# A decoder layer with 32 routed experts: the token lists computed by one-hot products, and the last shared sums stored from another queue

## The chip, the cores and the metric

One core of one Trainium2 chip runs the whole kernel. The metric is device time in microseconds (us). Times without a unit are microseconds from the start of the profiled span. TensorE is called PE, VectorE DVE, ScalarE ACT, GpSimd POOL and SyncE SP.

## What is computed

One decoder layer on 4096 tokens (2 x 2048) of width 512, in float32, in three residual steps. The first two are attention-like (stage 0 of the kernel: squared-relu scores against fixed weight keys; stage 1: cross-attention on 128 context tokens). The third is the one that matters here: a shared SwiGLU plus one of 32 routed SwiGLUs for each token.

```python
shared_out = silu(x @ sg) * (x @ su) @ sd            # 512 -> 1024 -> 512, all tokens
logits = x @ gate_w                                  # 32 experts
topk_ids = argmax(logits); scores = sigmoid(max(logits))
sorted_x = (x * scores)[argsort(topk_ids)]
d = grouped_mm(silu(grouped_mm(sorted_x, rg)) * grouped_mm(sorted_x, ru), rd)
out = x + shared_out + d[inverse order]
```

The number of tokens of each expert is known only when the kernel runs.

## The kernel before, in words

Every float32 matmul is done in fp32r as three products of rounded high and low parts (`three`). `split` (L89) makes the parts: ACT casts the high one (L94), and DVE or POOL subtracts for the low one (L97). The instructions of each engine stand in a fixed order, which a list scheduler decides when the kernel is built, with modelled costs. `later` shifts the priority of what is written inside it (positive: later). Tiles come from tagged slots in rotation (tags A to K, `raw` for loads, `W` with 45 slots); the first write of a tile waits until the users of the slot's former tile are done. PSUM has the banks P1 to P4, two buffers each.

The parts follow one another, with PE as the engine that is fed:

- **Stages 0 and 1** (to about 1450). Stage 1 writes for each token the index of its expert into `ef` (128 partitions x 32: token t*128+partition in column t), the scaled tokens `xs` to DRAM, and the residual `x2`.
- **Shared.** The first 1024 tokens go plainly (`plain_up`, `plain_down`). Three groups G of 1024 tokens follow, each in three steps p over 256 hidden columns, nine steps in all, of about 30 us each from 1511 on. A step does seven Strassen-like products (`up`, matmuls at L970). DVE adds the PSUM banks into `u` (L977, L980, L981) and `gu` (L991, L994), ACT applies silu, DVE multiplies by it (L958; one quarter is multiplied by POOL instead), and `split` gives hh and hl. After each product `between` gives one turn to several generators: the weights of the next step, splits of `z` and of the down weights, one `down` (L1002, bank P4) of the step before, which DVE adds into `acc` (L1008, slots W), and one stretch of `route` (it goes on at each `yield`). In the last step of a group `acc` is stored to `out` by SP's queue (L1010).
- **Route** (L623-772), inside the shared part. All values stand in 128 partitions x 32. `oh` is the token-by-expert table (128 x 32 x 32 bf16); five doubling additions give running sums; matmuls with a triangle and with ones (bank P4, L675, L681) give each token's place within its expert and the experts' totals. Experts are ranked by their number of tokens. Each rank has a fixed capacity `CAP` and first block `BASE`; what exceeds it goes to overflow blocks of 128. Tables of 128x1024 (L642, L644) and reductions over them (L648) select base, capacity, expert by rank and overflow offsets, which make up `plan` (97 integers that SP reads into registers: 32 experts by rank, 64 overflow experts, the number of overflow blocks). Operations of 128x512 (L731-741) and small ones (L744-755) give the address of each token. 32 indirect DMAs (L760, POOL) write the token numbers into four lists in DRAM, which four stores at the start had filled with 4096, a token that doesn't exist. SP loads the lists back (L767), DVE takes their minimum (L770), and `idx` (128 x blocks) and `ids` (its copy in DRAM for the overflow loop) are done.
- **Routed** with **Rest** woven in. Blocks of 256, 128 or 64 tokens of one expert: `gather` (L1192, an indirect DMA of POOL that reads `idx`) fetches `x` into slots of tag H, PE turns it (L1204; L1223 for blocks of 256), products (L1233, L1288), and an indirect DMA that adds into `out` (L1331). Weights are loaded by SP and split in `load` into rh and rl, whose slots are shared with `acc` (tag W). Rest does the last 256 hidden columns of the shared part (L1113, L1142) and adds its result `v` into `out` by POOL's queue (L1146).
- **Overflow** (L1416): a loop over the overflow blocks, its count from `plan[96]`.

Routed begins with these lines (L1385), where `blocks[0]` is Rest's first block and `blocks[1]` the first routed one, of 256 tokens, so two gathers:

```python
    with later(g, -200):
        prepare(*blocks[0])
        prepare(*blocks[1])
        turn_x(*blocks[0], "P3")
```

Of the kernel before, what the change touches and what calls it, by code (L numbers as in the profile page):

```python
# [8 lines left out]
F32 = mybir.dt.float32  # L9
FR = mybir.dt.float32r  # L10
# [25 lines left out]
NBLK = NB + NOV  # L36

# [585 lines left out]
def route(g, ef, tab, tri, lists, ids, plan, idx):  # L623
# [3 lines left out]

    room = []

    def small(name, dt=F32, n=E):  # L630
        if not room or room[-1][1] + n > 512:
            room.append([g.raw.tile([128, 512], F32, name="small", tag="raw"), 0])
        v, at = room[-1]
        room[-1][1] += n
        return v[:, at:at + n].bitcast(dt)
# [4 lines left out]
    def table(name, a, b, op, c=None, op2=None, tag="K"):  # L640
        w = big(name, tag)
        V.tensor_tensor(w[:], a, b, op)  # L642
        if c is not None:
            V.tensor_tensor(w[:], w[:], c, op2)  # L644
        return w

    def total(out, w):
        V.tensor_reduce(out, w, AX.X, A.add)  # L648

    consts = g.a.tile([128, 256], F32, name="consts", tag="m", bufs=2)  # L650
    nc.sync.dma_start(consts[:, 0:160], tab)
    iota, cst = consts[:, 0:64], consts[:, 64:160]
    io, basec, capc, tok = iota[:, 0:E], cst[:, 0:E], cst[:, E:2 * E], cst[:, 2 * E:3 * E]
    tri32 = g.tile("K", "tri32", F32, (128, 256))
    nc.sync.dma_start(tri32[:], tri)
    trib = g.tile("K", "trib", BF, (128, 256))
    V.tensor_copy(trib[:], tri32[:])

    yield

    oh = table("oh", bc(io, 1, E), bc(ef[:], 2, E), A.is_equal, tag="J")
# [7 lines left out]
    pos = [g.tile("G", "pos", F32, (128, 16, E)) for _ in range(2)]  # L669
    for hf in range(2):  # L670
        o = g.bank("P4", "rt", (128, 16, E))
        first = 1 - hf
        for w, x, t in ((0, oh, 0), (128, run, -1)):
            k = first if w else 0
            nc.tensor.matmul(o[:, k:, :].rearrange("p t e -> p (t e)"), trib[:, w:w + 128],  # L675
                             x[:, 16 * hf + t + k:16 * hf + 16 + t, :].rearrange("p t e -> p (t e)"),
                             start=w == 0, stop=w > 0, skip_group_check=True)
        nc.scalar.copy(pos[hf][:], o[:])
        yield
    o = g.bank("P4", "rt", (128, E))  # L680
    nc.tensor.matmul(o[:], trib[:, 128:256], run[:, E - 1, :], start=True, stop=True)  # L681
    tot, key, rank = small("tot"), small("key"), small("rank")
    V.tensor_copy(tot[:], o[:])
    yield

    V.tensor_scalar(key[:], tot[:], float(E), None, A.mult)
    V.tensor_tensor(key[:], key[:], io, A.subtract)
    total(rank[:], table("gt", bc(key[:], 1, E), bc(key[:], 2, E), A.is_gt)[:])
    yield
    ro = table("ro", bc(io, 1, E), bc(rank[:], 2, E), A.is_equal, tag="J")  # L690
    base, cap, er = small("base"), small("cap"), small("er")
    total(base[:], table("wb", ro[:], bc(basec, 1, E), A.mult)[:])
    total(cap[:], table("wc", ro[:], bc(capc, 1, E), A.mult)[:])
    yield
    total(er[:], table("we", ro[:].rearrange("p e r -> p r e"), bc(io, 1, E), A.mult)[:])
    V.tensor_copy(plan[:, 0:E], er[:])

    yield

    over, oi, nov = small("over"), small("oi", I32), small("nov", n=1)  # L700
    V.tensor_tensor(over[:], tot[:], cap[:], A.subtract)
    V.tensor_scalar(over[:], over[:], 0.0, 127.0, A.max, A.add)
    V.tensor_copy(oi[:], over[:])
    V.tensor_scalar(oi[:], oi[:], 7, None, A.arith_shift_right)
    V.tensor_copy(over[:], oi[:])
    total(nov[:], over[:])
    V.tensor_copy(plan[:, 96:97], nov[:])
    yield
    ovs, ove = small("ovs"), small("ove")
    total(ovs[:], table("lt", bc(io, 2, E), bc(io, 1, E), A.is_gt, bc(over[:], 1, E), A.mult)[:])  # L710
    V.tensor_tensor(ove[:], ovs[:], over[:], A.add)
    for hf in range(2):
        te = small(f"te{hf}")
        total(te[:], table("le", bc(iota[:, 32 * hf:32 * hf + 32], 2, E), bc(ove[:], 1, E), A.is_ge)[:])
        V.tensor_scalar(te[:], te[:], float(E - 1), None, A.min)
        yield
        V.tensor_copy(plan[:, 32 + 32 * hf:64 + 32 * hf], te[:])

    yield

    diff, blk, pt = small("diff"), small("blk"), small("pt")
    V.tensor_scalar(diff[:], ovs[:], float(NB), None, A.add)
    V.tensor_tensor(diff[:], diff[:], base[:], A.subtract)
    for hf in range(2):
        ts = slice(hf * 16, hf * 16 + 16)
        shape = [128, 16, E]
        capb, diffb, baseb = (v[:].unsqueeze(1).to_broadcast(shape) for v in (cap, diff, base))
        sel = g.tile("K", "sel", F32, (128, 16, E))
        past = g.tile("K", "past", F32, (128, 16, E))
        yield  # L730
        V.tensor_tensor(sel[:], pos[hf][:], capb, A.is_ge)  # L731
        V.tensor_tensor(past[:], sel[:], capb, A.mult)
        V.tensor_tensor(pos[hf][:], pos[hf][:], past[:], A.subtract)
        yield
        V.tensor_tensor(sel[:], sel[:], diffb, A.mult)
        V.tensor_tensor(sel[:], sel[:], baseb, A.add)
        V.tensor_tensor(sel[:], sel[:], oh[:, ts, :], A.mult)
        total(blk[:, ts], sel[:])
        yield
        V.tensor_tensor(pos[hf][:], pos[hf][:], oh[:, ts, :], A.mult)  # L740
        total(pt[:, ts], pos[hf][:])
    yield
    pi, hi = small("pi", I32), small("hi", I32)
    V.tensor_copy(pi[:], pt[:])  # L744
    V.tensor_scalar(hi[:], pi[:], 7, None, A.arith_shift_right)
    V.tensor_scalar(pi[:], pi[:], 127, None, A.bitwise_and)
    V.tensor_copy(pt[:], hi[:])
    V.tensor_tensor(blk[:], blk[:], pt[:], A.add)
    V.tensor_copy(pt[:], pi[:])
    V.tensor_scalar(pt[:], pt[:], float(NBLK), None, A.mult)  # L750
    V.tensor_tensor(blk[:], blk[:], pt[:], A.add)
    yield
    dst, toki = small("dst", I32), small("toki", I32)
    V.tensor_copy(dst[:], blk[:])
    V.tensor_copy(toki[:], tok)
    yield

    flat = [v[:].rearrange("p (b o) -> (p b) o", o=1) for v in lists]
    for t in range(E):
        nc.gpsimd.indirect_dma_start(out=flat[t % 4], out_offset=bass.IndirectOffsetOnAxis(ap=dst[:, t:t + 1], axis=0),  # L760
                                     in_=toki[:, t:t + 1], in_offset=None)
        if t % 2:
            yield
    parts = []
    for v in lists:
        parts.append(g.W.tile([128, NBLK], I32, name="list", tag="W"))
        nc.sync.dma_start(parts[-1][:], v[:])  # L767
    yield
    for v in parts[1:]:
        V.tensor_tensor(parts[0][:], parts[0][:], v[:], A.min)  # L770
# [784 lines left out]
```

## Time and profile before

| | us |
|---|---|
| median of three runs | 2704.23 (2700.75, 2704.23, 2708.0) |
| the profiled execution, its own time | 2703.28 |
| its span from first to last instruction | 2701.4 |
| mean granted clock of PE in it | 0.997 |
| routing on DVE: 73 instructions | 56.5 busy, mostly 1549-1641 |
| routing on POOL: 32 indirect DMAs | 31.4 busy, 1643-1722 |
| the list ready (`idx`) | 1725.3 |
| first gathers of routed tokens start | 1790.5, 1802.3, 1806.4, 1812.8 |
| the seam, from the last pair product to the first routed one | about 1800-1826 |

How the profile is read. A row of a group names line, engine, operation, tiles out<-in, shape and count, then busy time and the mean of one in ns. A row of a wait names the engine, what it wanted to do, after "<-" who released it, then the microseconds in total, how many times and the longest. "128x512 f32" is partitions x elements of a partition. A row of a timeline is start, duration, engine, line, operation; in brackets the idle time ahead of it and its releaser. An engine name with q (SPq) is that engine's instruction queue: DMA issues and semaphores. Matmul ends are modelled, so gaps on PE are best read from start to start.

The granted clock was 0.5 in three pieces of 3.413 us, at 1125.2, 1449.4 and 1824.9.

### The profile page before, as it was taken

To read this page: it belongs to the slowest core of one execution; us is meant where nothing else is said; L and a number is where in the kernel's file an instruction comes from. 1 tells how busy PE (TensorE), PEld (TensorE's weight loads), DVE (VectorE), ACT (ScalarE), POOL (GpSimd) and SP (SyncE) were. 2 spreads that over 40 slices of the span, in tenths; PEclk is the share of its full clock that TensorE was granted. 3 is DMA by queue.
4 is the path that set the end of the run, shared out by engine and by line. 5 is a ranking of instruction groups with operands and counts; after the bars stand their busy time and mean duration, and the time that the engine had idled before them with its cause. 6 is when DMAs were issued, how large, how long until landed. Compare 5 with 4: busy or idle time off the path is not lost. (4 is left out here: it accounts for less than half of the span.)

```text
span 2701.4 us, 47562 instructions
## 1 busy us (share of the span) xinstructions
PE 2641.7 (98%) x14629; PEld 2274.0 (84%) x14629; DVE 2071.4 (77%) x4703; ACT 1853.0 (69%) x4118; POOL 1132.2 (42%) x911
## 2 busy tenths in 40 slices
PE   7999999999999999999999999999999999999998
PEld 5878888887878999899997878778989898898886
DVE  7777777777777988888887487574777777778985
ACT  7788788888767777677785323343666676767885
POOL 5576565666644334344341457621122222212221
PEclk9999999999999999999999999999999999999999
DMA  4012112212021223323249846663889899999994
GB/s 154 32 63 86 55 67 81 81 47 76 30 87 34 80 76 130 103 92 107 79 143 338 289 142 238 218 211 108 261 282 281 281 305 299 295 284 291 323 319 148
DMA packets 269408, 446.66 MB, mean 165 GB/s; under 512 B 33536, under 2 KB 77568, under 8 KB 269152
## 3 DMA queue, kind: packets, MB, share of 16 engines
q1 hardware_dynamic: 254464, 416.46, 45.5%
q0 software_dynamic: 14688, 27.17, 4.9%
q8 instruction: 115, 1.88, 0.3%
q14 instruction: 141, 1.16, 0.1%
HBM read 348.83 MB, written 96.64 MB: 165 GB/s over the span
## 5 line engine op out<-in xcount | busy, mean ns | idle before, releaser
L97 DVE TENSOR_TENSOR rl<-raw,rh 128x512 fp32r<-128x512 f32 x768 | 487.7, 683 | 86.8 <-ACT rh L94 59.6
L94 ACT CAST rh<-raw 128x512 fp32r<-128x512 f32 x768 | 438.3, 621 | 138.5 <-DMA raw<-in_rg 89.2
L97 POOL TENSOR_TENSOR pl<-p,ph 128x512 fp32r<-128x512 f32 x320 | 411.3, 1296 | 263.2 <-ACT ph L94 206.5
L349 ACT ACTIVATE rl<-s 128x512 f32<-128x512 f32 x512 | 293.0, 604 | 38.1 <-PE s L345 32.8
L1331 POOL DMA_INDIRECT out_dram<-v,idx x46 | 114.7, 2492 | 457.7 <-ACT v L1329 367.4
L464 ACT ACTIVATE e<-e,nm 128x128 f32<-128x128 f32 x512 | 199.2, 391 | 70.4 <-DVE nm L461 70.1
L353 DVE TENSOR_TENSOR p<-s,rl 128x512 f32<-128x512 f32 x320 | 215.0, 682 | 40.6 <-ACT rl L349 38.2
L94 ACT CAST ph<-p 128x512 fp32r<-128x512 f32 x320 | 199.2, 626 | 63.1 <-DVE p L353 60.2
L467 POOL TENSOR_TENSOR e<-e,ri 128x512 f32<-128x512 f32 x128 | 133.2, 1042 | 215.0 <-DVE ri L465 103.3
L345 PE MATMUL s<-qh,kwl 128*128 128x512 f32 x512 | 205.7, 403 | 7.3 <-DVE p L353 4.1
L309 PE MATMUL o<-pl,vwh 128*128 128x512 f32 x512 | 202.8, 396 | 1.4 <-POOL pl L97 1.4
L309 PE MATMUL o<-ph,vwl 128*128 128x512 f32 x512 | 200.4, 393 | 0.9 <-ACT ph L94 0.9
L353 DVE TENSOR_TENSOR s<-s,rl 128x512 f32<-128x512 f32 x192 | 133.2, 694 | 88.3 <-ACT rl L349 87.8
L345 PE MATMUL s<-ql,kwh 128*128 128x512 f32 x512 | 200.1, 391 | 0.0
L345 PE MATMUL s<-qh,kwh 128*128 128x512 f32 x512 | 199.9, 390 | 0.0
L309 PE MATMUL o<-ph,vwh 128*128 128x512 f32 x512 | 199.7, 390 | 0.0
L970 PE MATMUL gu<-z,swh 128*128 128x512 f32 x504 | 157.3, 389 | 0.0
L438 PE MATMUL q<-yh,wql 128*128 128x256 f32 x512 | 149.5, 292 | 2.8 <-DVE v L497 2.4
L97 DVE TENSOR_TENSOR pl<-s,ph 128x512 fp32r<-128x512 f32 x192 | 131.0, 683 | 20.6 <-ACT ph L94 18.2
L438 PE MATMUL q<-yh,wqh 128*128 128x256 f32 x512 | 145.6, 284 | 0.0
L438 PE MATMUL q<-yl,wqh 128*128 128x256 f32 x512 | 145.0, 283 | 0.0
L97 POOL TENSOR_TENSOR vl<-v,vh 128x512 fp32r<-128x512 f32 x64 | 84.4, 1319 | 124.3 <-ACT vh L94 111.6
(361 smaller groups left out, 7996.1 us busy)
## 6 DMA issues: line engine op xcount, KB each, us to landing
raw<-in_rg SPq DMA_DIRECT2D x256, 256.0 KB
raw<-in_ru SPq DMA_DIRECT2D x256, 256.0 KB
raw<-in_rd SPq DMA_DIRECT2D x256, 256.0 KB
z<-zT SPq DMA_DIRECT2D x116, 256.0 KB
b<-x SPq DMA_DIRECT2D x40, 256.0 KB
raw<-in_sgu SPq DMA_DIRECT2D x39, 256.0 KB
swh<-wS SPq DMA_DIRECT2D x36, 256.0 KB
swl<-wS SPq DMA_DIRECT2D x36, 256.0 KB
```

Source lines behind the costliest of these rows:

```text
L94: g.nc.scalar.copy(hi, src)
L97: g.low = (lo_engine or g.nc.vector).tensor_tensor(lo, src, f32(hi), A.subtract)
L309: nc.tensor.matmul(o[:], w, y[:], start=kt == 0 and n == 0, stop=kt == 15 and n == 2)
L345: nc.tensor.matmul(s[:], w, y[:], start=n == 0, stop=n == 2)
L349: m0 = nc.scalar.activation(r[:], s[:], AF.Relu)
L353: m1 = nc.vector.tensor_tensor(p[:], s[:], r[:], A.mult)
L438: nc.tensor.matmul(o[:, i, :], part(w, k, p), y[k // 2][:, k % 2, :], start=n == 0, stop=n == 11)
L464: nc.scalar.activation(e[:, hs], e[:, hs], AF.Exp, bias=nm[:, h:h + 1], scale=0.125, accum_out=su[:, h:h + 1])
L467: nc.gpsimd.tensor_tensor(e4, e4, ri[:].unsqueeze(2).to_broadcast([128, 4, 128]), A.mult)
L970: nc.tensor.matmul(o[:], y, z, start=(at, x) not in begun, stop=j == 1 and m == 2, skip_group_check=True)
L1331: nc.gpsimd.indirect_dma_start(out=out, out_offset=bass.IndirectOffsetOnAxis(ap=idx[rows, b + j:b + j + 1], axis=0), in_=v[rows], in_offse ...
```

## The change

Four edits, in `route`, `down`, `gather` and the constants:

1. **Values by expert in 32 partitions.** Totals are made in two forms, as a row in all partitions and as a column of 32 partitions (two small matmuls). Rank, capacity, base, overflow are then [32,1] values or [32,32] tables; overflow offsets come from a matmul with the triangle. `plan` is made from one PSUM tile by a minimum (128x96) and one copy.
2. **One packed look-up.** Capacity, 8 x base and 512 x d (the distance to the overflow block) are put on the diagonals of three 32x32 bf16 tables and summed by three accumulated matmuls with ones into one row; each token picks its value by one 128x512 product with `oh` and a reduction for each half, and shifts and masks take it apart.
3. **Lists as one-hot products.** For each of 32 columns of tokens DVE makes `lt` (128x128: is this the token's slot?) and `rt` (128x128: is this its block? times the token's code), both in fp32r; PE multiplies them into P4, four columns in one accumulation, eight of these in all; DVE adds each 128x110 result into `acc`. A few more operations turn code into token number. The 32 indirect DMAs, the lists in DRAM, their loads and the four stores at the start are gone.
4. **Queue and slot.** The eight stores of the last group's `acc` go to POOL's queue; the gather of `blocks[1]` takes a slot of tag F instead of H.

The order of instructions is the same on every engine to the end of stage 1, but for SP's four stores and POOL's memset at the start. In the changed order the one-hot operations on DVE stand in one run of 16 and then in runs of 8. The diff, cut to its core (code that only goes is left out where the description above tells it; the constants too):

```diff
+    iota, capc, basec, code, own = (consts[:, a:b] for a, b in ((0, 128), (128, 160), (160, 192), (192, 224), (224, 225)))
+    io = iota[:, 0:E]
     tri32 = g.tile("K", "tri32", F32, (128, 256))
     nc.sync.dma_start(tri32[:], tri)
-    trib = g.tile("K", "trib", BF, (128, 256))
-    V.tensor_copy(trib[:], tri32[:])
-
+    tables = g.tile("G", "tables", BF, (128, 1024))
+    trib, ones = tables[:, 0:128], tables[:, 128:256]
+    V.tensor_copy(tables[:, 0:256], tri32[:])
+
+    ecol, ro, over_b, ge = (tables[0:E, a:b] for a, b in ((256, 384), (384, 416), (416, 448), (448, 512)))
+    diag = [tables[0:E, 512 + 32 * i:544 + 32 * i] for i in range(3)]
+    V.tensor_copy(ecol, own[0:E].to_broadcast([E, 128]))
...
+    of_all = g.bank("P4", "rt", (128, 64))
+    product(of_all[:, 0:E], ones, run[:, E - 1, :])
+    product(of_all[0:E, E:E + 2], run[:, E - 1, :], ones[:, 0:2])
+
+    tot, key, rank = (small(n, n=1, p=E) for n in ("tot", "key", "rank"))
+    keys, gt = (small(n, p=E) for n in ("keys", "gt"))
+    V.tensor_copy(tot, of_all[0:E, E:E + 1])
+    V.scalar_tensor_tensor(key, tot, float(E), own[0:E], A.mult, A.subtract)
+    V.scalar_tensor_tensor(keys, of_all[0:E, 0:E], float(E), io[0:E], A.mult, A.subtract)
+    V.tensor_tensor(gt, keys, key.to_broadcast([E, E]), A.is_gt)
+    total(rank, gt)
+    V.tensor_scalar(ro, io[0:E], rank, None, A.is_equal)
...
+        pos = g.tile("G", "pos", F32, (128, 16, E))
+        V.tensor_tensor(pos[:], o[:], oh[:, ts, :], A.mult)
+        total(pt[:, ts], pos[:])
...
+    cap, base, over, oi, ove, d = (small(n, n=1, p=E) for n in ("cap", "base", "over", "oi", "ove", "d"))
+    V.tensor_tensor(keys, ro, capc[0:E], A.mult)
+    V.tensor_tensor(gt, ro, basec[0:E], A.mult)
+    total(cap, keys)
+    total(base, gt)
+    V.scalar_tensor_tensor(over, cap, -64.0, tot, A.mult, A.add)
+    V.tensor_scalar(over, over, 0.0, 127.0, A.max, A.add)
+    oi = oi.bitcast(I32)
+    V.tensor_copy(oi, over)
+    V.tensor_scalar(oi, oi, 7, None, A.arith_shift_right)
+    V.tensor_copy(over, oi)
+    V.tensor_copy(over_b, over.to_broadcast([E, E]))
...
+    product(of_all[0:E, 0:E], trib[0:E, 0:E], over_b)
+    ovs = small("ovs", n=1, p=E)
+    V.tensor_copy(ovs, of_all[0:E, 0:1])
+    V.tensor_tensor(ove, ovs, over, A.add)
+    V.tensor_scalar(ge, iota[0:E, 0:64], ove, None, A.is_ge)
+    V.scalar_tensor_tensor(d, ovs, float(NB + 64), base, A.add, A.subtract)
+    for v, col, w in zip(diag, (cap, base, d), (1.0, 8.0, 512.0)):
+        V.tensor_scalar(v, g.ident[0:E, 0:E], col, w, A.mult, A.mult)
+    o = g.bank("P4", "rt", (128, 160))
+    product(o[:, 0:32], ecol, ro)
+    product(o[:, 32:96], ones[0:E], ge)
+    product(o[:, 96:98], ones[0:E], over_b[:, 0:2])
+    for i, v in enumerate(diag):
+        product(o[:, 128:160], ones[0:E], v, i, 2)
+    V.tensor_scalar(plan[:, 0:96], o[:, 0:96], float(E - 1), None, A.min)
+    V.tensor_copy(plan[:, 96:97], o[:, 96:97])
+
+    rec = small("rec")
+    for hf in range(2):
+        ts = slice(16 * hf, 16 * hf + 16)
+        sel = g.tile("G", "sel", F32, (128, 16, E))
+        V.tensor_tensor(sel[:], oh[:, ts, :], o[:, 128:160].unsqueeze(1).to_broadcast([128, 16, E]), A.mult)
+        total(rec[:, ts], sel[:])
...
+    ri, parts, blk = small("ri", I32), small("parts", I32, 3 * E), small("blk")
+    V.tensor_copy(ri, rec)
+    V.tensor_scalar(parts[:, 0:32], ri, 7, 6, A.bitwise_and, A.logical_shift_left)
+    V.tensor_scalar(parts[:, 32:64], ri, 3, 63, A.logical_shift_right, A.bitwise_and)
+    V.tensor_scalar(parts[:, 64:96], ri, 9, None, A.logical_shift_right)
+    pf = small("pf", n=3 * E)
+    V.tensor_copy(pf, parts)
+    past = rec
+    V.tensor_tensor(past, pt, pf[:, 0:32], A.is_ge)
+    V.scalar_tensor_tensor(blk, pf[:, 64:96], -64.0, past, A.add, A.mult)
+    V.tensor_tensor(past, past, pf[:, 0:32], A.mult)
+    V.tensor_tensor(pt, pt, past, A.subtract)
+    V.tensor_tensor(blk, blk, pf[:, 32:64], A.add)
+    at, atf = parts[:, 0:64], pf[:, 0:64]
+    V.tensor_copy(ri, pt)
+    V.tensor_scalar(at[:, 0:32], ri, 7, None, A.arith_shift_right)
+    V.tensor_scalar(at[:, 32:64], ri, 127, None, A.bitwise_and)
+    V.tensor_copy(atf, at)
+    V.tensor_tensor(blk, blk, atf[:, 0:32], A.add)
+    slot = atf[:, 32:64]
...
-    flat = [v[:].rearrange("p (b o) -> (p b) o", o=1) for v in lists]
-    for t in range(E):
-        nc.gpsimd.indirect_dma_start(out=flat[t % 4], out_offset=bass.IndirectOffsetOnAxis(ap=dst[:, t:t + 1], axis=0),
-                                     in_=toki[:, t:t + 1], in_offset=None)
-        if t % 2:
-            yield
-    parts = []
-    for v in lists:
-        parts.append(g.W.tile([128, NBLK], I32, name="list", tag="W"))
-        nc.sync.dma_start(parts[-1][:], v[:])
-    yield
-    for v in parts[1:]:
-        V.tensor_tensor(parts[0][:], parts[0][:], v[:], A.min)
-    V.tensor_copy(idx[:], parts[0][:, 0:NB])
-    nc.sync.dma_start(ids[:], parts[0][:])
+    acc = g.W.tile([128, NBLK], F32, name="list", tag="W")
+    for c in range(8):
+        lt, rt = g.tile("J", "lt", FR, (128, 4, 128)), g.tile("K", "rt", FR, (128, 4, 128))
+        with later(g, 30):
+            for i in range(4):
+                t = slice(4 * c + i, 4 * c + i + 1)
+                V.tensor_scalar(lt[:, i, :], iota, slot[:, t], None, A.is_equal)
+                V.tensor_scalar(rt[:, i, :], iota, blk[:, t], code[:, t], A.is_equal, A.mult)
+        yield
+        with later(g, 30):
+            o = g.bank("P4", "rt", (128, 128))
+            for i in range(4):
+                product(o[:], lt[:, i, :], rt[:, i, :], i, 3)
+            if c == 0:
+                V.tensor_copy(acc[:], o[:, 0:NBLK])
+            else:
+                V.tensor_tensor(acc[:], o[:, 0:NBLK], acc[:], A.add)
+        yield
+    none = g.W.tile([128, NBLK], F32, name="none", tag="W")
+    V.tensor_scalar(none[:], acc[:], 0.0, float(T - 2047), A.is_equal, A.mult)
+    V.scalar_tensor_tensor(acc[:], acc[:], 0.0, acc[:], A.is_lt, A.add)
+    out = g.W.tile([128, NBLK], I32, name="out", tag="W")
+    V.scalar_tensor_tensor(out[:], acc[:], 2047.0, none[:], A.add, A.add)
+    V.tensor_copy(idx[:], out[:, 0:NB])
+    nc.sync.dma_start(ids[:], out[:])
...
-            nc.sync.dma_start(out[r, :], b[:])
+            (nc.gpsimd if G == NG - 1 else nc.sync).dma_start(out[r, :], b[:])
...
-    def gather(b, r, m):
+    def gather(b, r, m, tag="H"):
-            x = g.tile("H", "x")
+            x = g.tile(tag, "x")
...
-        prepare(*blocks[1])
+        prepare(*blocks[1], "F")
...
-                empty = g.tile("A", "empty", I32, (128, NBLK))
-                nc.gpsimd.memset(empty[:], T)
-                for v in lists:
-                    nc.sync.dma_start(v[:], empty[:])
```

## The prediction

> **What bounds the kernel now.** I read the busy shares first.
>
> ```profile
> PE 2641.7 (98%) x14629; PEld 2274.0 (84%) x14629; DVE 2071.4 (77%) x4703; ACT 1853.0 (69%) x4118; POOL 1132.2 (42%) x911
> ```
>
> PE is the bound, and the change takes no matmul out of it. It can win only where PE stood still, and it loses what it adds to PE. So the second view is PE's waits, from the first routing step (1580) to just behind the seam between the shared and the routed part (1860).
>
> ```profile
> PE pt L1204 <- DMA x<-xs,idx: 2.1, 1, 2.1
> PE gu L970 <- DVE u L977: 2.1, 1, 2.1
> PE d L1002 <- DVE acc L1008: 2.0, 2, 1.2
> PE pt L1223 <- DVE acc L1008: 1.9, 2, 1.3
> PE d L1002 <- ACT hh L94: 1.8, 1, 1.8
> PE gu L970 <- DVE u L981: 0.8, 1, 0.8
> ```
>
> They are small and lie in three places. I price each by the gap between the starts of neighbouring matmuls less the usual pitch (0.227 us for 512 columns, 0.119 for 256), which also finds stops too short for the list: 6.0 us in 1590-1625, 3.5 in 1709-1726, 7.1 in 1800-1850, under 1 elsewhere between 1500 and 1850. That makes some 17 us, the ceiling of any gain. The third view says who is full there (columns: us, then PE, PEld, DVE, ACT, POOL busy, granted clock, DMA share, GB/s).
>
> ```profile
> 1590.00:1625.00 35.00, 30.94 (x129) 23.33 (x128) 34.97 (x51) 9.56 (x18) 17.60 (x13) 1.00 0.41 129
> ...
> 1645.00:1709.00 64.00, 64.00 (x284) 52.98 (x283) 35.66 (x55) 19.42 (x34) 58.38 (x52) 1.00 0.72 249
> 1709.00:1726.00 17.00, 14.16 (x61) 10.92 (x59) 5.94 (x12) 3.67 (x7) 12.55 (x12) 1.00 0.14 39
> ...
> 1800.00:1850.00 50.00, 45.99 (x310) 42.34 (x308) 23.12 (x37) 15.23 (x27) 8.51 (x8) 0.97 0.57 177
> ```
>
> In the first stretch DVE has no free microsecond (34.97 of 35): routing's arithmetic sits on it. In the second POOL is full (58.38 of 64). At the seam nobody is full: there it is transfers.
>
> **Part 1: matmuls added.** 32 one-hot products of 128 columns, and 9 of 2 to 96 columns; the four position products stay, the one of the totals becomes two of the nine. The nearest row is the kernel's 128-column transposes, whose starts lie 0.109 us apart; by the pitch of the wide ones (0.227 for 512, 0.119 for 256) 128 columns would take 0.065. So 32 x 0.065 = 2.1 to 32 x 0.109 = 3.5, and the small ones 8 net x 0.04 to 0.09, 0.3 to 0.7. PE has no slack: all of it counts. I take the transposes, since each product also has fresh weights as they have: **+4.2** (2.4 to 4.2).
>
> **Part 2: routing's arithmetic on DVE.** Before, it is 73 instructions, 56.5 us; the comparison with the experts, the five doubling adds and the cast of the triangle (4.4 us) stay, so 52.1 us go. In their place: 64 `tensor_scalar` of 128x128. The free 128x32 costs 0.17 (L745, L750) and the free 128x512 0.52 (L160), so 0.24 each, 15.4 us. About 44 small ones at 0.17, 7.5. Four 128x512 products at 0.68 and four reductions at 0.67, 5.4. Eight additions of 128x110, 0.25 each, 2.0. Together 30.3 us. That free price is not what the trace mostly shows:
>
> ```profile
> 1589.58 1.32 DVE L703 CAST small<-small 128x32 int32<-128x32 f32 x1
> ...
> 1592.07 1.33 DVE L755 CAST small<-consts 128x32 int32<-128x32 f32 x1
> 1593.32 1.32 DVE L705 CAST small<-small 128x32 f32<-128x32 int32 x1
> ```
>
> and POOL in the same microseconds:
>
> ```profile
> 1589.56 1.30 POOL L97 TENSOR_TENSOR dwl<-raw,dwh 128x512 fp32r<-128x512 f32 x1
> ...
> 1592.07 1.30 POOL L97 TENSOR_TENSOR dwl<-raw,dwh 128x512 fp32r<-128x512 f32 x1
> 1593.32 1.28 POOL L97 TENSOR_TENSOR z<-zs,z 128x512 fp32r<-128x512 f32 x1
> ```
>
> Each cast ends where POOL's operation ends: 1.32 instead of the 0.17 that L744 and L747 take with POOL idle. The Trainium skill, "SBUF — State Buffer", section "Who interferes with whom", has the rule, and it speaks against this change: copy, cast and tensor_scalar can take the port pair that DVE shares with GpSimd, and whoever issues first holds it for the whole instruction. The change trades few wide operations, which lose little by it, for some 110 narrow ones that each may wait a POOL operation. By the free row the added work is 30.3 us; by the rule at its worst (a POOL operation always running, each one-hot waiting 1.30) the 64 alone take 64 x 1.30 = 83 us. No trace here shows a `tensor_scalar` that writes fp32r, so whether this form takes the pair is open. By L722 (1.31 beside POOL, writing f32) I assume that it does. How often is POOL running? In 1645-1726 it is busy 70.9 us, some 30 of them list DMAs that go: 41 of 81 us, half. A burst beside a half-busy POOL lasts twice its free time, so 0.48 us for each one-hot, 31 us for all.
>
> Has DVE room? PE reaches the eight list products about 10.0 us of its own work apart, from some 84 to 154 us behind the first product of the pairs (which begin at 1511), so about 1595 to 1665. Per 10 us DVE has about 5.5 us of other work (35.66 in 64) and a 0.25 addition, which leaves 4.25 for eight one-hots, 0.53 each. At 0.48 they just fit. They are issued in bursts of eight (16 in the first), several right ahead of L977 and L980, whose u then comes late, and behind those the split L97, the `down` matmuls and `acc`; PE's products of the list wait for them too, with the pair products queued behind. Some lateness stays: I take 3 us for the one-hots and 3 for the small ones, which still fall in the six z splits of POOL at 1588-1602. That equals the 6.0 of before: **0** (from -5, if the form leaves the pair alone, to +14, see the second rival).
>
> **Part 3: lists.** 32 indirect DMAs, 31.4 us of POOL, go:
>
> ```profile
> L760 POOL DMA_INDIRECT list<-small x32: 954/977/1211, 1643.3 to 1720.9; - x32
> ```
>
> They cost PE twice. POOL, full to 1723, makes u (L958) late, ACT waits 6.2 us for it at hh, and PE 1.96 at 1710. Then the minima on DVE wait 8.2 us for the list loads with an `acc` behind them, and PE loses 1.32 at 1724. Next late at 1710 would be ACT's own hh, which has over 4 us of slack; at 1724 the `acc` itself, 0.7 us. **-3.5** (-3.5 to -2). That the list is ready 60 us earlier is worth nothing more: the gathers wait for slots, not for it. SP loses four loads (7.8 us of waiting in its queue) but gets its reads of the plan as a block, 23 in a row at 0.59 = 14 us (before at most 16, 1611.1-1620.6). Queued behind them are z and swh/swl, needed over 10 us later: 0, up to +2 without that cover. The four stores and the memset at the start: PE's first wait, 12.1 us, hangs on xt, its statistics and y, not on the weights behind the stores: 0 (-0.5 to 0).
>
> **Part 4: the seam.** Block 1's gather no longer waits for an H slot, so the 2.1 us of L1204 go (2.28 with the pitch): **-2.3** (-2.3 to 0, if F comes free no earlier). The eight last stores go from SP's queue to POOL's. SP issues one in 0.35 us; the same kind on POOL's queue (L1146) takes 0.985:
>
> ```profile
> L1010 SPq DMA_DIRECT2D out_dram<-acc x8: 332/350/1077, 1808.0 to 1825.0; - x8
>   ACT rh L94: 14.3, 4
>   DVE rl L97: 8.2, 3
> ```
>
> ```profile
> L1146 POOL DMA_DIRECT2D out_dram<-v x32: 888/985/1306, 1816.3 to 2495.9; - x32
> ```
>
> ACT's rh and DVE's rl wait for the slots that these stores release, and DVE has an `acc` queued behind rl, for which PE waits at L1223 (1.35 + 0.75 in starts). SP issued each store at most 1 us behind its `acc`; POOL adds 0.6 of issue, and its queue has gathers and the Rest part's v store between, the latter waiting for ACT, which waits at rh. Against it: the 2.3 us gained bring the middle ones forward. From -3.7 (these stops gone with the 1.6 us that PE loses at half clock at 1824.9) to +4: I take 0, since both ends are a shift of the same wait.
>
> **Sum.** +4.2 + 0 - 3.5 - 2.3 = -1.6 us on the profiled execution's 2703.28 (span 2701.4 and 1.9 around it), so 2701.7. It lies 0.95 under the median of 2704.23: **2702.6** in its terms. Without the surprises of the rivals I hold 2696 to 2709 likely.
>
> **Rivals.** *The stalls go* (0.22): the one-hots write fp32r without taking the pair, 0.24 each, and routing's stall falls from 6 to 1, -5; the seam is mended whole, -2.3 - 3.7 with the half clock; the lists -3.5; PE's addition at 3.2. Sum -11.3: **2693**. For it: DVE's free work falls by 22 us. Against it: the port rows.
> *One-hots held by POOL* (0.28): over 0.53 us each DVE falls behind. That is the deciding point: POOL busy over 55% of a burst (0.24/0.45 = 0.53), and I expect half. If three of the eight chunks meet POOL back to back, as it runs at 1588-1602, each takes 8 x 1.30 + 5.75 = 16.2 us for 10.0; 6.2 late, 1.5 of that absorbed in slack, 3 x 4.7 = +14. Sum +12.4: **2716.6**. Against it: such runs of POOL last 15 us in a step of 30.
> *Stores block the seam* (0.10): POOL's queue delays each slot by a gather and a v store, and L1223 waits 4 us more; the longer stop also costs 1 us more of half clock. -1.6 + 4 + 1: **2707.6**. *The lists were cover* (0.06): PE's stops at 1710 and 1724 only move to the next releaser, -1 instead of -3.5: 2705. The sum as it stands has 0.34.
>
> **Chances.** A difference of 0.3%, 8.1 us, is about what a measurement of this kernel can tell from no change: 2696.1 and 2712.3. Faster by more 0.22 (the first rival), slower by more 0.26 (most of the second), within 0.52. For 8 in 10 the range takes in the middle of both outer cases and some 3 us beyond, for a fourth chunk held or a further stop gone: 2690 to 2720.
>
> **What would show it.** Part 1: the starts of the list products 0.109 apart, not 0.065. Part 2: mean of the one-hot rows, 0.48 (0.24: first rival; over 0.53 with PE waiting for DVE in 1590-1700: second). Part 3: no PE stop between 1700 and 1730. Part 4: L1204 without a wait on x, and what L1223, rl and rh wait for. I am wrong if PE stops over 12 us between 1580 and 1720, or if a part that the change leaves alone (before 1450) moves.

## The result, and the profile after

The changed kernel takes 2707.54 us in the median of 19 runs (2703.61 to 2710.1), the kernel before 2703.21 in 19 runs beside it (2699.36 to 2708.0): ratio 1.0014, 95% interval 1.0007 to 1.0020, so 3.8 us slower (1.9 to 5.4). That is within the range and within 0.3%, but not in the direction forecast (-1.6). A second set of 21 runs gave 1.0011 (1.0005 to 1.0018). The profiled execution took 2707.75 us, its span 2705.9. The changed `route` has 13 to 14 lines more, so L970 of before is L983 now, L1002 is L1015, L1008 is L1021, L97 is L98, L1204 is L1218.

PE is as full as before, with 40 matmuls more (busy time, share, instructions).

```profile
PE 2647.6 (98%) x14669; PEld 2278.5 (84%) x14669; DVE 2074.8 (77%) x4762; ACT 1853.8 (69%) x4116; POOL 1101.4 (41%) x886
```

PE's waits between 1580 and 1860:

```profile
PE d L1015 <- DVE acc L1021: 3.7, 1, 3.7
PE gu L983 <- DVE hl L98: 2.9, 2, 2.1
PE rt L645 <- DVE acc L1021: 1.6, 1, 1.6
PE g L1302 <- ACT th L95: 0.3, 1, 0.3
PE g L1302 <- DVE tl L98: 0.2, 1, 0.2
PE gu L983 <- DMA swl<-wS: 0.2, 1, 0.2
```

The waits for x, for u and for ACT's hh at 1710 are gone. In their place are one of 3.7 us behind `acc` (at the seam, 1813), one of 2.1 behind hl (at 1617) and one of 1.6 in front of the first list product. The four stretches of before (columns as there):

```profile
1590.00:1625.00 35.00, 31.14 (x133) 24.65 (x132) 34.71 (x68) 13.73 (x25) 19.49 (x16) 0.95 0.68 241
1645.00:1709.00 64.00, 63.06 (x284) 51.79 (x283) 36.37 (x70) 21.93 (x40) 30.27 (x25) 1.00 0.63 227
1709.00:1726.00 17.00, 17.00 (x77) 14.08 (x76) 7.97 (x13) 4.87 (x9) 8.76 (x7) 1.00 0.62 200
1800.00:1850.00 50.00, 45.85 (x302) 41.54 (x302) 23.38 (x37) 15.77 (x28) 10.14 (x14) 0.97 0.63 192
```

1709-1726 is mended: PE 17.00 of 17. In 1590-1625 DVE is as full as it was (34.71 of 35), with 68 instructions where there were 51, and the clock there fell to 0.95: one piece of 3.413 us at half, at 1619.4, which before had none in this stretch.

The ledger below sums, for each kernel's profile, the gaps between starts of neighbouring matmuls less the usual pitch (half clock included); the matmuls of routing stand apart with their whole time. "Routing" is 190 us from the first pair product, "lists" from there to the last pair product, "seam" from there to 24 us behind the first product of a routed block.

| kernel | ratio to before (95%) | routing's matmuls | routing | lists | seam | sum |
|---|---|---|---|---|---|---|
| before | | 0.6 | 7.0 | 3.8 | 7.0 | 18.4 |
| changed | 1.0014 (1.0007 to 1.0020) | 4.9 | 10.9 | 0.1 | 7.6 | 23.5 |
| changed, again | 1.0011 (1.0005 to 1.0018) | 4.9 | 10.6 | 0.1 | 7.5 | 23.1 |
| stores on SP | 0.9999 (0.9990 to 1.0007) | 4.4 | 8.3 | 0.1 | 8.1 | 20.9 |
| stores on SP, again | 1.0004 (0.9998 to 1.0011) | 4.4 | 7.4 | 0.1 | 5.1 | 17.0 |
| routing alone | 1.0016 (1.0008 to 1.0024) | 4.5 | 11.5 | 0.2 | 9.4 | 25.6 |
| before + POOL stores | 1.0007 (0.9998 to 1.0015) | 0.6 | 7.1 | 3.6 | 8.4 | 19.7 |
| before + slot F | 0.9998 (0.9989 to 1.0006) | 0.6 | 7.1 | 4.4 | 7.7 | 19.8 |
| lists late | 1.0010 (1.0003 to 1.0016) | 4.3 | 13.9 | 0.4 | 4.8 | 23.4 |
| lists late, SP | 1.0021 (1.0011 to 1.0030) | 4.3 | 11.0 | 0.4 | 6.5 | 22.2 |
| quarter of one-hots and products | 0.9975 (0.9966 to 0.9983) | 1.7 | 3.8 | 0.1 | 9.6 | 15.2 |
| quarter of one-hots | 0.9975 (0.9966 to 0.9984) | 4.3 | 3.7 | 0.3 | 8.6 | 16.9 |
| wide one-hots | 0.9995 (0.9986 to 1.0003) | 4.3 | 5.6 | 0.1 | 6.4 | 16.4 |
| wide one-hots, SP | 0.9994 (0.9985 to 1.0002) | 4.3 | 5.3 | 0.1 | 6.8 | 16.5 |

One line is one profiled execution; the ratio is from all runs. Ahead of these columns executions differ by up to 5.8 us by themselves, since the half-clock pieces before the shared part come and go (the first pair product starts between 1508.0 and 1513.8).

Two things limit what one profile can tell. A stop of about 1 us some 10 us behind the first pair product (at 1518 in the changed kernel, behind ACT's hh of the plain part) stands ahead of everything new in routing (on DVE that begins at 1519.7). It comes and goes: the first profile with stores on SP has it and the second does not, the kernel before with slot F has it and the kernel before does not. It makes up 1.0 to 1.3 of the routing column where it occurs. And the seam of one and the same kernel, stores on SP, lost 8.1 and 5.1. So 1.3 us in routing, or 3 us at the seam, between two single profiles is no evidence by itself.

### The profile page after: what moved, and what is told of

It is laid out like the page before. It is cut to its first block, busy times and chain, and to the rows that moved or that the text cites. A ratio compares the mean times of both kernels' runs of the same rounds, so it can differ in the third digit from the quotient of the medians.

```text
span 2705.9 us, 47634 instructions
## 1 busy us (share of the span) xinstructions
PE 2647.6 (98%) x14669; PEld 2278.5 (84%) x14669; DVE 2074.8 (77%) x4762; ACT 1853.8 (69%) x4116; POOL 1101.4 (41%) x886
## 5 line engine op out<-in xcount | busy, mean ns | idle before, releaser
L98 DVE TENSOR_TENSOR rl<-raw,rh 128x512 fp32r<-128x512 f32 x768 | 488.8, 684 | 88.8 <-ACT rh L95 62.4
L98 POOL TENSOR_TENSOR pl<-p,ph 128x512 fp32r<-128x512 f32 x320 | 411.6, 1297 | 263.1 <-ACT ph L95 210.6
L983 PE MATMUL gu<-z,swh 128*128 128x512 f32 x504 | 157.9, 392 | 0.0
L98 DVE TENSOR_TENSOR pl<-s,ph 128x512 fp32r<-128x512 f32 x192 | 131.1, 683 | 20.8 <-ACT ph L95 18.3
L98 POOL TENSOR_TENSOR vl<-v,vh 128x512 fp32r<-128x512 f32 x64 | 84.5, 1320 | 124.4 <-ACT vh L95 119.7
```

Source lines behind the costliest of these rows:

```text
L98: g.low = (lo_engine or g.nc.vector).tensor_tensor(lo, src, f32(hi), A.subtract)
L983: nc.tensor.matmul(o[:], y, z, start=(at, x) not in begun, stop=j == 1 and m == 2, skip_group_check=True)
```

## The experiments

**Which edit costs?** The routing alone, without the two edits at the seam:

```diff
-            (nc.gpsimd if G == NG - 1 else nc.sync).dma_start(out[r, :], b[:])
+            nc.sync.dma_start(out[r, :], b[:])
...
-        prepare(*blocks[1], "F")
+        prepare(*blocks[1])
```

> The changed kernel with both edits at the seam undone (slot H, stores by SP): the new routing alone. Theory: products +4.35, stops in the routing stretch +3 to +4.5, lists -3.6, seam unchanged: 3 to 5 us above the kernel before. Rival (the time lost is lost at the seam): within 1 us of the kernel before.

Measured: 1.0016, 4.3 us above the kernel before (2.2 to 6.5). The rival, that the time is lost at the seam by the two edits, falls: the new routing carries the loss alone. The seam was expected to be unchanged. In the one profile it rises from 7.0 to 9.4, and DVE's order there is another one: a rl that waits for a store of `acc` (6.25 us in front of it, until 1822.7) stands ahead of two `acc`. The size of this rise lies within what two profiles of one kernel differ.

**What in the routing?** First a quarter of the list work, one-hots and products:

```diff
-            for i in range(4):
+            for i in range(1):
                 t = slice(4 * c + i, 4 * c + i + 1)
...
-            for i in range(4):
-                product(o[:], lt[:, i, :], rt[:, i, :], i, 3)
+            for i in range(1):
+                product(o[:], lt[:, i, :], rt[:, i, :])
```

> The changed kernel with only the first of each four columns in the lists (16 one-hots and 8 products instead of 64 and 32); it leaves three quarters of the tokens out of the lists, whose places stay padding, while all blocks are computed as before. Products: 24 x 0.112 = 2.7 us less on PE. Theory: the stops in the routing stretch go as well, 10.9 to about 5, so about 2707.5 - 2.7 - 5.5 = 2699.5. Rival (the one-hots on DVE cost PE nothing): 2704.8.

Then a quarter of the one-hots with all products (the loop over products again 4 long, each `product(o[:], lt[:, 0, :], rt[:, 0, :])`):

> The changed kernel with one-hots for the first of each four columns only, but all 32 products, each of which overwrites the one before with the same operands; three quarters of the tokens are left out of the lists. It splits what the quarter kernel saved (9.9 us against the changed kernel) between PE's products and DVE's one-hots. Theory: the one-hots on DVE cost PE 7 us through its stops, so 4.5 to 5 us below the kernel before. Rival: the products are the price, and it stands at the kernel before or above.

Both stand at 0.9975, 6.8 us below the kernel before. The clearer reading is in the ledger: routing's loss is 10.9 us with 64 one-hots and 3.8 and 3.7 with 16, whether PE does 8 products (1.7 us of matmuls) or 32 (4.3). So the one-hots cost PE some 6 to 7 us by stops, the products 2.6 by their own time; the rival falls. The times themselves are not clean: with three quarters of the tokens missing most rows of the routed blocks are padding, which may lighten the accumulating DMAs too. The ledger explains 3.2 and 1.5 of the 6.8 us, and the two times don't show the 2.6 us between them.

The routing column, by its distance from the first pair product (us lost; the same sums, within 0.1 of the ledger):

| kernel | 0-25 | 25-79 | 79-116 | 116-190 |
|---|---|---|---|---|
| before | 0.0 | 0.6 | 6.2 | 0.1 |
| before + slot F | 1.3 | 0.6 | 5.1 | 0.1 |
| changed | 1.3 | 1.3 | 6.3 | 1.9 |
| changed, again | 1.3 | 1.3 | 6.3 | 1.6 |
| quarter of one-hots and products | 0.0 | 1.3 | 0.4 | 2.1 |
| quarter of one-hots | 1.1 | 1.3 | 0.3 | 0.9 |
| wide one-hots | 0.0 | 1.3 | 1.7 | 2.5 |

The third stretch (1587-1625 in the changed kernel) holds the first three bursts of one-hots: nearly all that is lost there is theirs, 6.3 against 0.3 and 0.4. Yet the kernel before lost as much there, by its own small operations. What the changed kernel loses more lies outside: 1.3 in the first, the stop that comes and goes without the new routing too; 0.7 in the second, short stops of 0.1 to 0.2 us around routing's small matmuls; and 1.8 in the fourth, half of it one stop at 1679 on an hl that waited for ACT's hh. With a quarter of the one-hots and products the fourth has 2.1, so it does not follow their number; its cause stays open.

**How one-hots stop PE.** The rows of the two kinds in the changed kernel (min/median/max ns), and then the worst burst on DVE and POOL beside it:

```profile
L767 DVE TENSOR_SCALAR lt<-consts,small x32: 273/278/1325, 1590.6 to 1655.8; 128x128 fp32r<-128x128 f32 x32
L768 DVE TENSOR_SCALAR rt<-consts,small x32: 334/338/1341, 1591.1 to 1656.0; 128x128 fp32r<-128x128 f32 x32
```

```profile
1611.91 1.08 DVE L767 TENSOR_SCALAR lt<-consts,small 128x128 fp32r<-128x128 f32 x1
1612.91 1.33 DVE L768 TENSOR_SCALAR rt<-consts,small 128x128 fp32r<-128x128 f32 x1
1614.17 1.32 DVE L767 TENSOR_SCALAR lt<-consts,small 128x128 fp32r<-128x128 f32 x1
1615.41 1.34 DVE L768 TENSOR_SCALAR rt<-consts,small 128x128 fp32r<-128x128 f32 x1
1616.67 1.31 DVE L767 TENSOR_SCALAR lt<-consts,small 128x128 fp32r<-128x128 f32 x1
...
1618.61 0.68 DVE L98 TENSOR_TENSOR hl<-gu,hh 128x512 fp32r<-128x512 f32 x1
```

```profile
1611.62 2.55 POOL L98 TENSOR_TENSOR z<-zs,z 128x512 fp32r<-128x512 f32 x2
1614.13 1.28 POOL L98 TENSOR_TENSOR swl<-raw,swh 128x512 fp32r<-128x512 f32 x1
1615.37 2.54 POOL L98 TENSOR_TENSOR dwl<-raw,dwh 128x512 fp32r<-128x512 f32 x2
```

Each of five one-hots ends where one of POOL's five operations ends, within 0.1 us. The burst of eight takes 6.7 us from start to start; free it would take 1.8 (consecutive starts lie 0.20 and 0.26 apart where POOL is idle). The split hl stands behind it, and PE waits 2.1 us for hl; the half clock follows. By the trace 13 of the 64 waited (7 lt, 6 rt), about 1 us each; all 64 together took 31.8 us (15.2 for lt, 16.6 for rt).

Not all of the loss is waiting for POOL. The stop in front of the first list product is on an `acc` that stands behind the first run of 16 one-hots:

```profile
1596.20 0.68 DVE L1021 TENSOR_TENSOR acc<-d,acc 128x512 f32<-128x512 f32 x1
```

```profile
1596.93 0.66 PE L645 MATMUL rt<-rt,lt 128*128 128x128 f32 x4 [1.60 <-DVE acc L1021]
```

That run takes 5.7 us (1590.55-1596.20). Two of the 16 waited for POOL, some 2 us; the other 3.7 are its own work.

How the same instructions run without and with POOL beside them can be seen where two kernels place POOL's splits differently. In the changed kernel POOL stands idle from 1588.2 to 1591.5:

```profile
1588.32 0.19 DVE L746 TENSOR_TENSOR small<-small 128x32 f32<-128x32 f32 x1
1588.55 0.19 DVE L747 SCALAR_TENSOR_TENSOR small<-small 128x32 f32<-128x32 f32 x1
1588.77 0.19 DVE L748 TENSOR_TENSOR small<-small 128x32 f32<-128x32 f32 x1
```

In the kernel of the next experiment, with the lists moved, POOL runs splits without a break there:

```profile
1588.45 1.20 DVE L746 TENSOR_TENSOR small<-small 128x32 f32<-128x32 f32 x1
1589.68 1.22 DVE L747 SCALAR_TENSOR_TENSOR small<-small 128x32 f32<-128x32 f32 x1
1590.92 1.21 DVE L748 TENSOR_TENSOR small<-small 128x32 f32<-128x32 f32 x1
```

```profile
1589.55 1.29 POOL L98 TENSOR_TENSOR dwl<-raw,dwh 128x512 fp32r<-128x512 f32 x1
1590.80 2.51 POOL L98 TENSOR_TENSOR swl<-raw,swh 128x512 fp32r<-128x512 f32 x2
```

**Moving the lists to a quieter place.**

```diff
+    for _ in range(16):
+        yield
     acc = g.W.tile([128, NBLK], F32, name="list", tag="W")
     for c in range(8):
```

> The changed kernel with 16 empty turns of the generator ahead of the one-hot lists, so that they come about 65 us later, in steps where POOL has fewer operations. Theory: PE's loss in the routing stretch (10.9 us between 1500 and 1700, with the half clock at 1619) comes from bursts of one-hots that POOL holds up while DVE is full; it falls to 6 or less, no half clock at 1619, time 5 us lower, about 2702.5. Rival: the loss follows the one-hots wherever they are (DVE has too much to do in any step), or belongs to the small operations: it stays at 9 or more and the time within 2 us of 2707.5.

> Both edits together: lists 16 turns later and the last stores on SP's queue, the gather still in slot F. Theory: both gains add, 2707.5 - 5 - 3 = 2699.5, below the kernel before (2703.2). Rival (neither stop has the cause named): 2707; if only one of the two holds, 2702.5 or 2704.5.

Both miss: 2.7 us and 5.7 us above the kernel before. The edit did not do what it should. The first two chunks were still placed at 1597 to 1600 (their slots are free), only the other six went to 1662-1719; and the splits of POOL now fall on the small operations, as shown above, which puts a stop of 4.7 us at 1592 in front of `down`. And the place was not quieter: one chunk met POOL back to back, so that all eight of its one-hots were held.

```profile
1682.87 1.29 DVE L769 TENSOR_SCALAR lt<-consts,small 128x128 fp32r<-128x128 f32 x1
1684.08 1.33 DVE L770 TENSOR_SCALAR rt<-consts,small 128x128 fp32r<-128x128 f32 x1
...
1691.61 1.30 DVE L770 TENSOR_SCALAR rt<-consts,small 128x128 fp32r<-128x128 f32 x1
1692.83 1.27 DVE L1023 TENSOR_TENSOR acc<-d,acc 128x512 f32<-128x512 f32 x2
```

This chunk took 10.0 us and cost PE a stop of 2.0 at 1691, with a half clock behind it (1693.9). So the experiment speaks neither for nor against a quieter place; it shows that the small operations can be hit as the one-hots are.

**Fewer, wider instructions.**

```diff
-            for i in range(4):
-                t = slice(4 * c + i, 4 * c + i + 1)
-                V.tensor_scalar(lt[:, i, :], iota, slot[:, t], None, A.is_equal)
-                V.tensor_scalar(rt[:, i, :], iota, blk[:, t], code[:, t], A.is_equal, A.mult)
+            four = [128, 4, 128]
+            i4 = iota.unsqueeze(1).to_broadcast(four)
+            s4, b4, c4 = (v[:, 4 * c:4 * c + 4].unsqueeze(2).to_broadcast(four) for v in (slot, blk, code))
+            V.tensor_tensor(lt[:], i4, s4, A.is_equal)
+            V.tensor_tensor(rt[:], i4, b4, A.is_equal)
+            V.tensor_tensor(rt[:], f32(rt[:]), c4, A.mult)
```

> The changed kernel with each chunk's eight one-hots of 128x128 made as three tensor_tensor of 128x512 with broadcast operands (24 instructions in place of 64; free work 24 x 0.68 = 16.3 us in place of 64 x 0.31 = 19.7). Theory: what costs is the number of narrow instructions that can wait 1.3 us for a POOL operation, 13 of 64 in the changed kernel; with 24 it is 5 or 6, each also shorter against its own length, and PE's loss in the routing stretch falls from 10.9 to 7 or less: 3 to 4 us below the changed kernel. Rival (DVE's total work in these steps is what counts): 1 us or less below it.

> The same wide one-hots with the last stores on SP's queue, gather in slot F. Theory: with the gain of the wide ones and what the stores on SP gave (0 to 4 us), 1 to 5 us below the kernel before, the first version that beats both kernels. Rival: at the changed kernel with SP stores, 0 to 2 us above the kernel before.

Measured 0.9995 and 0.9994 beside 1.0011 for the changed kernel in the same set: 0.0016 and 0.0017 of 2704, so 4.3 and 4.6 us below it. Routing's loss falls to 5.6 and 5.3, most of it in the third stretch (6.3 to 1.7). The expectation took the free work to fall too, by durations, but consecutive durations overlap. From start to start it is the same: 14.5 us for 64 narrow ones (0.196 and 0.256) and 14.4 for 24 wide ones (0.60). With the waits they hold DVE for 27.0 and 22.4 us, so what went is waiting, and the rival (DVE's total work) falls. 8 of the 24 waited, more than the 5 or 6 expected. The burst that held hl is the plainest case, three waits in place of five, 4.8 us in place of 6.7:

```profile
1609.87 1.50 DVE L768 TENSOR_TENSOR lt<-consts,small 128x512 fp32r<-128x512 f32 x1
1611.29 1.78 DVE L769 TENSOR_TENSOR rt<-consts,small 128x512 fp32r<-128x512 f32 x1
1613.11 1.67 DVE L770 TENSOR_TENSOR rt<-rt,consts 128x512 fp32r<-128x512 f32 x1
1614.70 0.68 DVE L1023 TENSOR_TENSOR acc<-d,acc 128x512 f32<-128x512 f32 x1
```

POOL's own splits wait beside the wide ones in turn: two took 3.46 us there, where two took 2.55 beside the narrow ones (1611.62).

PE's waits of the wide kernel between 1560 and 1860:

```profile
PE gu L985 <- ACT dwh L95: 1.8, 1, 1.8
PE d L1017 <- DVE acc L1023: 1.6, 1, 1.6
PE gu L985 <- DVE u L995: 1.2, 1, 1.2
```

The stops on hl and ahead of the list products are gone. The order on the other engines moved with this edit, so not all of the gain need be the number of waits. Both versions have lower medians than the kernel before (2702.75 and 2701.82 beside 2704.5), but their intervals against it still hold 1, so neither is shown to beat it.

**The seam.** Slot F alone in the kernel before (the edit of the change), and the POOL stores alone in it:

> The kernel before with only the gather of the first routed block in slot F. Theory: the wait for the gather ran beside the wait of DVE's rl for a slot; with the gather early PE stops instead behind acc, which stands behind rl: no wait on x, a stop of about 2 to 3 us on acc in its place, loss at the seam still 6.5 us or more, time within 1.5 us of the kernel before. Rival (the prediction's step): the 2.3 us go, loss 5.0, time 2.3 us below.

> The kernel before with only the eight last stores moved to POOL's queue. Theory (stores land later from this queue: 6.3 us after issue for the first in the changed kernel, against some 4 on SP): PE's loss at the seam rises from 7.3 us by 0.5 to 2, time 1 us above the kernel before. Rival (the queue of the stores doesn't matter, since PE waits there for the gather first): loss and time the same within 0.5 and 1 us.

Slot F shows no gain: 0.9998 (0.9989 to 1.0006), though this interval reaches down to -3.0 us and does not exclude the forecast -2.3. The profile says more. In the kernel before, DVE waited at the seam at the same time as PE waited for x (1809.6 to 1811.9):

```profile
1809.89 0.68 DVE L1008 TENSOR_TENSOR acc<-d,acc 128x512 f32<-128x512 f32 x1
1812.82 0.70 DVE L97 TENSOR_TENSOR rl<-raw,rh 128x512 fp32r<-128x512 f32 x1 [2.24 <-DMA out_dram<-acc]
1814.17 0.69 DVE L1008 TENSOR_TENSOR acc<-d,acc 128x512 f32<-128x512 f32 x1 [0.66 <-PE d L1002]
```

With the gather early (before + slot F) the wait on x is gone, PE's waits there are others, and the loss is 7.7 where 7.0 was and 4.7 was forecast. One stop of 2 to 3 us on `acc` was expected; it came as several of about 1 us or less:

```profile
PE d L1142 <- ACT hh L94: 0.9, 1, 0.9
PE d L1002 <- DVE acc L1008: 0.9, 1, 0.9
PE g L1288 <- ACT th L94: 0.8, 1, 0.8
PE pt L1223 <- DVE acc L1008: 0.6, 2, 0.4
```

In the changed kernel the same wait has become one stop. The DVE order puts rl, which waits for the first store, ahead of an `acc`:

```profile
1811.40 0.68 DVE L1142 TENSOR_TENSOR s<-u,s 128x512 f32<-128x512 f32 x1
1815.92 0.69 DVE L98 TENSOR_TENSOR rl<-raw,rh 128x512 fp32r<-128x512 f32 x1 [3.84 <-DMA out_dram<-acc]
1816.53 0.68 DVE L1021 TENSOR_TENSOR acc<-d,acc 128x512 f32<-128x512 f32 x1
```

```profile
1809.53 0.62 POOL L1024 DMA_DIRECT2D out_dram<-acc  x1 [7.50 <-DVE acc L1021]
```

From the issue of that store to rl are 6.4 us on POOL's queue (6.1 in before + POOL stores), 4.8 on SP's in the kernel before. Over all profiles, seven with each queue, the time from the first store to the rl that waits for it is 5.1 to 7.0 us on POOL's queue (mean 6.2) and 3.7 to 5.9 on SP's (mean 4.9). POOL stores alone give 1.0007 (0.9998 to 1.0015), 1.9 us, which just doesn't exclude nothing; the seam rose by 1.4, as expected, but within its scatter. The reverse, stores back on SP with slot F kept:

> The changed kernel with the eight last stores of acc back on SP's queue; PE's and DVE's instructions stand in the same order. Theory: the first stores on POOL's queue land 6 to 7 us after their issue, DVE's rl waits for the slot (3.84 us), acc stands behind it, and PE stops 3.83 us at 1813 with half clock after it. On SP the stop falls to 1.5 or less and the loss of PE at the seam (gaps between matmul starts over the usual pitch, half clock included) from 7.8 to 4.5 us or less; time 3 us below the changed kernel, about 2704.5. Rival: the earlier gather only brings PE sooner to the same wait for slots, whoever stores; the loss stays at 7 or more and the time at 2707.5.

> The changed kernel once more, beside its twin with the stores on SP. Their first times lie 4 us apart, though the loss at the seam in their profiles is the same (7.6 and 8.1 us), and the difference in the profiles is the stop at 1617 with its half clock, which the twin lacks with the same order on PE and DVE. If the queue decides (the prediction's third rival in part), it stays 3.5 to 4 us above the kernel before and shows the stop at 1617; if that stop comes and goes by chance, it may be missing here, and the time lies 1.5 to 4 us above.

> The changed kernel with the last stores on SP's queue once more. Queue decides: within 1 us of the kernel before, no stop at 1617. Chance: 1 to 3 us above the kernel before, and the stop at 1617 may show.

Stores on SP stand at 0.9999 and 1.0004, the changed kernel at 1.0014 and 1.0011: some 3 us between them. But the first profile with SP stores does not show the cause that was expected: its seam still loses 8.1 with a stop of 3.1 on the same rl, 5.9 us behind an SP store. The second loses 5.1, with a stop of 1.9 and 4.7 us behind the store, near what was expected. What differs in both pairs of profiles is the stop at 1617: 2.2 us in both of the changed kernel, none in both with SP stores, though PE and DVE have the same order. In the latter the half clock follows the stop at 1595 already (1598.3 and 1602.1, not 1619.4 and 1619.6); ACT is later, and POOL's last split starts at 1619.1, behind the burst:

```profile
1615.89 1.28 POOL L98 TENSOR_TENSOR dwl<-raw,dwh 128x512 fp32r<-128x512 f32 x1
1619.10 1.29 POOL L98 TENSOR_TENSOR dwl<-raw,dwh 128x512 fp32r<-128x512 f32 x1 [1.93 <-ACT dwh L95]
```

The routing alone has SP stores and has the stop at 1617, so the queue isn't a sufficient reason for its absence. Besides, up to the seam PE, DVE, ACT and POOL have the same order in all four profiles, and the first store that the edit moves is issued at 1806.9 or later, 190 us behind the stop. The routing column (10.9 and 10.6 against 8.3 and 7.4) holds 2.9 us on average, about the whole difference in time. Whether the queue has a part in it, or the stop falls with the half clock by chance, stays open.

## Why the prediction was wrong

The forecast was -1.6. The ledger has +4.3, +3.9, -3.7 and +0.6 for the four parts, together 5.1; less the 1.3 of the stop at 1518, which comes and goes with either routing, 3.8. The times say 3.8 (1.9 to 5.4). Two steps failed, of about the same size: the gain at the seam in part 4, and in part 2 the zero outside its own stretch.

- **Part 1** was right: routing's matmuls went from 0.6 to 4.9 us, +4.3 for +4.2. 0.4 of it is half clock. Within a group of four the starts of list products lie mostly 0.110 to 0.114 us apart, as the transposes' do.
- **Part 3** was right: no stop of PE between 1700 and 1730, 3.7 us gone.
- **Part 4 failed** in "so the 2.1 us of L1204 **go**". The wait on x did go, but the seam lost 7.6 and 7.5 us in the two profiles of the changed kernel, and 7.7 with slot F alone, where 7.0 less 2.3 was forecast: +0.6 in place of -2.3. The prediction saw that rl waits for the stores and priced it as a second, separate item at 0. It ran beside the gather's wait, so the gather had been its cover: next late was `acc` behind rl, with as much as the 2.3 us. The issue of a store by POOL was forecast at 0.985 from L1146 and took 0.57: L1146 accumulates into `out`, the moved stores don't. What the queue does is to free the slot some 1.3 us later on average; whether PE pays for it is not shown.
- **Part 2 failed** in "That equals the 6.0 of before: **0**", +3.9 in the ledger. In the stretch that the 6.0 was read from it came true (6.3 for 6.2), and that was luck: of "3 us for the one-hots and 3 for the small ones" the one-hots cost 6 and the small ones at most 0.4, since POOL stood idle beside most of them. What failed in the sum is that it put nothing elsewhere: 0.7 came ahead of this stretch and 1.8 behind it. The cause of the 1.8 stays open. The other 1.3 is the stop at 1518.
- In the mechanism of part 2, what failed is that the one-hots "just fit". It compared a mean with a mean. The total on DVE was forecast well (31 us, measured 31.8), but for other reasons: free ones took 0.28 and 0.34, not 0.24, and 13 of the 64 waited, most of them for about a whole POOL operation. Five of the 13 stood in a row: a burst of 6.7 us, with hl behind it, and PE ran out of work. The mean of 0.50 lay below the named deciding point of 0.53, and PE stopped all the same. The second rival had the mechanism, at three held chunks and +14; one was held for most of its length, two others in part.
- The rule that the prediction took from the Trainium skill ("SBUF — State Buffer", section "Who interferes with whom") held: the wait ends with POOL's operation, and the `tensor_scalar` that writes fp32r is subject to it (1.31 to 1.34 us, where 0.34 is free). Its worst case for all 64 (83 us) was as far off as the free price (15).

## What to carry to other kernels

Small DVE instructions beside a busy POOL should be counted, not only timed: a burst lasts as long as the POOL operations that it meets. Making the same values in fewer, wider instructions gave back 4.3 us here. Placing a burst by the longest run of POOL, not by POOL's mean share, is what the traces suggest; the one try at moving it did not test it. When a wait is removed, list every other wait that ends within the same microseconds: what ran beside it is what is late next. When a sum comes out right in total, look at its terms: here 3 + 3 was 6 + 0.4. And an edit in one stage can reorder another: the new routing alone gave DVE another order at a seam 150 us later. What that cost is not known from one profile.

## What was not expected of the hardware

- A `tensor_scalar` of 128x128 into fp32r took 0.28 us with one column of scalars and 0.34 with two, and consecutive ones started 0.20 and 0.26 us later.
- A 128x32 operation with both inputs in SBUF took 0.19 us with POOL idle and 1.20 to 1.22 with POOL's splits running beside it.
- The plain store on POOL's queue issued in 0.57 us (0.54 to 0.64) where the accumulating store on the same queue (L1160) takes 0.96.
- The clock can fall to half for 3.413 us behind a stop of PE of only 1.76 us (two profiles), but it did not behind the same stop in three others, nor behind one of 2.27 in the kernel before (at 1595). The Trainium skill ("TensorE: Matmul & The Clock Gate", section "What's actually happening") tells of a free-running window of 3413 ns and of an idle window of about that length before the clock falls: the length of the piece agrees, the need for a whole idle window does not. What decides it the runs don't show.
